# Two banded layers on one core: the second bias added in the first layer's pass, variance work off VectorE, GpSimd's chain in pieces, an order for each layer

## The chip, the cores and the metric

The kernel runs on one core of a Trainium2 chip. The metric is device time in microseconds, the median of several executions. All data is float32.

## The reference

Two layers with the same structure and weights of their own follow each other. Each normalises its input by groups of two channels over the whole 512 x 512 picture, runs a gated banded product over it, and adds the result to its input.

```python
def _ref(x, ...):                     # x: (1, 512, 512, 64)
    xn = _ln(x, norm_scale, norm_bias)
    left = (xn @ Wl + bl) * mask * sigmoid(xn @ Wlg + blg)      # 64 -> 128
    right = (xn @ Wr + br) * mask * sigmoid(xn @ Wrg + brg)
    out_gate = sigmoid(xn @ Wog + bog)
    out = _banded_ingoing(left, right, 4)     # out[i, j] = sum over |d| <= 4 of left[i+d, i] * right[i+d, j]
    out = _ln(out, out_norm_scale, out_norm_bias) * out_gate
    return out @ Wo + bo                                        # 128 -> 64

x = x + _ref(_gn(x), layer 0's weights)   # _gn: mean and variance of each pair of channels
x = x + _ref(_gn(x), layer 1's weights)
```

## The kernel before

First comes a pass over x for the group statistics (`input_stats`), during which the weights of both layers are prepared (`solve_layer`). Then `layer` runs twice, from x to mid_x and from mid_x to out, with `mid_stats` between them, which turns sums gathered on TensorE during the first layer (`sums`) into the second layer's group statistics.

The picture is cut into 9 blocks of 64 rows that overlap by the band, and each block into 2 chunks of columns, so 18 chunks. A chunk has 16 steps, and each step takes one unit of 64 rows x 8 columns in each half of the picture (128 partitions, tile z). A layer has 288 steps of projections, and 288 of outputs, which lag 30 steps behind (`LAG`).

What a unit passes through: it is loaded (`load`), scaled by ga and moved by gb (`affine`, GpSimd), its mean and variance are taken (`inner_stats`, VectorE), it is centred and rescaled (`inner_norm`, GpSimd), transposed on TensorE (`transposed`), evacuated to zT by ScalarE (`kept`), and projected twice (`right`, TensorE; `right_gate`, a sigmoid on ScalarE; `right_end`, a product on VectorE into RO). When a chunk's RO is filled, `mix` multiplies it with the band matrices A on TensorE, in 16 pieces per chunk, and each piece is copied back to RO by one ScalarE and one VectorE copy. Then come the statistics of the outputs (`out_stats`, VectorE), their normalisation (`norm`, eight ScalarE activations of 128x128 per step), the turn to channels on partitions (`turned`, TensorE), the product with the gate (`gates`, `gated`, `times_gate`), the last product with Wo (`end`), and the sum with the residual row XR (`ended`, VectorE). Before that sum, GpSimd has added the layer's bias to XR (`biased`).

Every fourth step `solve` turns the variances gathered since into reciprocal roots: VectorE prepares the variances in tile var, with four small instructions, and makes a first guess in rs by integer arithmetic (`rsqrt`'s first instruction, called the seed here); GpSimd then refines it in ten small instructions, and two more give each output's scale and shift.

All engines keep program order (`InOrder`): each engine executes its instructions in the order in which the loop in `layer` issues them. The loop issues a step's parts in one fixed order, the same for both layers. Two tables spread the uneven work over 16 steps: `count` says how many units GpSimd scales and moves in each step, and `step` gives the band products, two, one or none to a step:

```python
step = [t0 + n for n, k in enumerate((2, 1, 2, 2, 1, 2, 1, 2, 2, 1)) for _ in range(k)]
count = [1, 1, 2, 1, 2, 1, 1, 2, 1, 1, 1, 0, 1, 1, 0, 0]
```

[...] In both layers a pool of two double banks (`two_banks`) serves the projections and the transposes; single banks (`one_bank`) serve the gates, the turn, the last product and the bands: three of them in the first layer, where one more bank gathers the sums, and four in the second. DMAs of the loop are issued from SyncE.

Of the kernel before, what the change touches and what calls it, by code (L numbers as in the profile page):

```python
# [30 lines left out]
LN_EPS = 1e-6  # L31

# [47 lines left out]
def tile_two_banded_layers(  # L80
# [35 lines left out]
    nc.vector.memset(all_ones, 1.0)  # L116
    ones_row = const.tile([1, P], F32, name="ones_row")
# [16 lines left out]
    def rsqrt(o: bass.AP, v: bass.AP, vec=nc.vector, e=nc.vector):  # L134


        p, n = v.shape
        t, u = (
            sm.tile([P, 3 * NB], F32, tag=f"rsqrt{i}", name="rsqrt", bufs=1)[:p, :n]
            for i in range(2)  # L140
        )
        vec.tensor_scalar(
            o.bitcast(I32), v.bitcast(I32), -0.5, float(0x5F3759DF), ALU.mult, ALU.add
        )
        e.tensor_tensor(t, o, o, ALU.mult)
        e.tensor_tensor(t, t, v, ALU.mult)
        e.tensor_scalar(u, t, -10.0 / 3.0, None, ALU.add)
        e.tensor_tensor(t, t, u, ALU.mult)
        e.tensor_scalar(t, t, 5.0, None, ALU.add)
        e.tensor_tensor(o, o, t, ALU.mult)  # L150
        e.tensor_tensor(t, o, o, ALU.mult)
        e.tensor_tensor(t, t, v, ALU.mult)
        e.tensor_scalar(t, t, -27.0 / 1024.0, 0.5625, ALU.mult, ALU.add)
        e.tensor_tensor(o, o, t, ALU.mult)


    PARTS = (
        ("right", 2 * H), ("left", 2 * H), ("gate", H), ("Wo", D), ("ob", 1), ("add", 2 * D),
# [60 lines left out]
    def solve_layer(i: int, f: dict, r: dict, tmp, half: bass.AP):  # L219
# [36 lines left out]
        add = r["add"].rearrange("p (t c) -> p t c", c=D)  # L256
        nc.vector.tensor_copy(add[:, 0, :], pb[:, :D])
# [15 lines left out]
        nc.vector.tensor_tensor(r["m2"], r["m"], r["m"], ALU.mult)  # L273

# [7 lines left out]
    def shifted(i: int, r: dict, tmp):  # L282
        add = r["add"].rearrange("p (t c) -> p t c", c=D)
        if i == 0:

            bias = tmp.tile([P, G], F32, name="bias")
            nc.vector.tensor_reduce(
                bias, add[:, 0, :].rearrange("p (g t) -> p g t", t=2), AX.X, ALU.add
            )
            nc.vector.scalar_tensor_tensor(bias, bias, 0.5, total, ALU.mult, ALU.add)  # L290
            spread(shift, bias)
        op = ALU.add if i else ALU.subtract
        nc.vector.tensor_tensor(add[:, 0, :], add[:, 0, :], shift, op)
        nc.vector.tensor_copy(add[:, 1, :], add[:, 0, :])


# [6 lines left out]
    shift = const.tile([P, D], F32, name="shift")  # L303
# [4 lines left out]
    def group_affine(mean: bass.AP, var: bass.AP, pool):  # L308

        ve = pool.tile([P, D], F32, name="g_ve")  # L310
        nc.vector.tensor_scalar(ve, var, GN_EPS, None, ALU.add)
        rsqrt(ga, ve)
        nc.vector.scalar_tensor_tensor(gb, mean, -1.0, ga, ALU.mult, ALU.mult)
# [113 lines left out]
    def affine(u: Unit, engine):  # L427

        engine.tensor_tensor(u.z, u.z, mid(ga, JU), ALU.mult)
        engine.tensor_tensor(u.z, u.z, mid(gb, JU), ALU.add)  # L430
# [5 lines left out]
    def inner_norm(u: Unit):  # L436
        z = u.z.rearrange("p (k t) c -> p k t c", t=2)
        m = u.mean.unsqueeze(3).broadcast_to([P, JU // 2, 2, D])
        en.gpsimd.tensor_tensor(z, z, m, ALU.subtract)
        en.gpsimd.tensor_tensor(u.z, u.z, last(u.rs, D), ALU.mult)  # L440
# [126 lines left out]
    def mix(c: int, A: bass.AP, h0: int) -> list:  # L567
# [6 lines left out]
        ph = [one_bank().rearrange("i (h t j) -> i h t j", h=q, t=2) for s in range(2)]  # L574
# [23 lines left out]
    def solve(w: dict, ins: list, outs: list, sti, sto):  # L598
# [3 lines left out]
        r = sm.tile([P, 3 * NB], F32, tag="rs", name="rs", bufs=3)[:, : ni + no]  # L602
        if ni:
            en.vector.tensor_scalar(
                v[:, :ni].rearrange("p (k t) -> p k t", t=2), sti[:, : ni // 2, 2::3],
                1.0 / D, LN_EPS, ALU.mult, ALU.add,
            )
            for n, u in enumerate(ins):
                u.rs = r[:, n * JU : (n + 1) * JU]
        if no:  # L610
# [3 lines left out]
            en.vector.scalar_tensor_tensor(  # L614
                vo.rearrange("p (k t) -> p k t", t=2), sto[:, :, 2::3], 1.0 / H,
                w["m2"][:, js].rearrange("p (k t) -> p k t", t=2), ALU.mult, ALU.mult,
            )
            en.vector.tensor_scalar(vo, vo, LN_EPS, None, ALU.add)
            nm = sm.tile([P, NB], F32, tag="nm", name="nm")[:, :no]
            en.vector.tensor_scalar(  # L620
                nm.rearrange("p (k t) -> p k t", t=2), sto[:, :, 1::3], -1.0, None, ALU.mult
            )
        rsqrt(r, v, en.vector, en.gpsimd)
        if no:
            ro = r[:, ni:]
            en.gpsimd.tensor_tensor(ro, ro, w["m"][:, js], ALU.mult)
            en.gpsimd.tensor_tensor(nm, nm, ro, ALU.mult)
            for n, o in enumerate(outs):
                o.rs, o.nm = ro[:, n * JU : (n + 1) * JU], nm[:, n * JU : (n + 1) * JU]

    def norm(o: Out, lo: int, hi: int):
        if lo == 0:
            o.on = onp.tile([P, JU, H], F32, tag="on", name="on")
        for j in range(lo, hi):
            en.scalar.activation(
                o.on[:, j, :].rearrange("p (h t) -> p h t", t=2), RO[:, :, o.c + j, :],
                AF.Identity, bias=o.nm[:, j : j + 1], scale=o.rs[:, j : j + 1],
            )
# [59 lines left out]
    def biased(o: Out, w: dict, stats: bool):  # L698
        n = S + o.blk.m
        f = o.xr[:n, :, 1 : 1 + 2 * D]  # L700
        add = fewer if stats and o.blk.m < S - WIN else w["add"]
        en.gpsimd.tensor_tensor(f, f, mid(add[:n], JU // 2), ALU.add)

    def end(o: Out, w: dict):
        m = o.blk.m
# [33 lines left out]
    def layer(src: bass.AP, dst: bass.AP, w: dict, stats: bool, then=None):  # L739
# [59 lines left out]
        A, sti, sto, then_affine = {}, {}, None, []  # L799
        for t in range(min(loads), last_t + 3):  # L800
# [21 lines left out]

            mixing, mixed = mixes.get(t, []), []
# [10 lines left out]

# [3 lines left out]
            for v in looking[0:3]:  # L838
                out_stats(*v)
            for u in inputs(t + 2):  # L840
                inner_norm(u)
            if t in units:
                right(units[t], 0, w)
            if t in units:
                right_gate(units[t], 0)
            if t in outs:
                gates(outs[t], w)
            if t in units:
                right(units[t], JQ, w)
            for u in affines.pop(t, []):  # L850
                affine(u, en.vector if u.at < NU + 4 else en.gpsimd)
            if t % 4 == 0 and t > NU:
                then_affine = affines.pop(t + 1, [])
            for v in looking[3:5]:
                out_stats(*v)
            for v in looking[5:]:
                out_stats(*v)
            for v in todo:
                inner_stats(*v)
            if t % 4 == 0:  # L860
                st, us = sti.pop((t + 4) // 4, (None, []))
                so, os = sto or (None, [])
                sto = None
                if us or os:
                    solve(w, us, os, st, so)
            if t in outs:
                gated(outs[t])
            if t in units:
                right_end(units[t], 0)
            if t in outs:  # L870
                biased(outs[t], w, stats)
            if t in outs:
                turned(outs[t], w)
            if t in units:
                right_gate(units[t], JQ)
            for u in inputs(t + 1):
                transposed(u)
            if t in outs:
                times_gate(outs[t], w)
            for u in then_affine:  # L880
                affine(u, en.gpsimd)
            then_affine = []
            if t - 1 in outs:
                end(outs[t - 1], w)
            if t in units:
                right_end(units[t], JQ)
            if len(mixing) > 0:
                c, h0 = mixing[0]
                mixed.append(mix(c, A[c, h0 // HA], h0))
            if t + 1 in outs:  # L890
                norm(outs[t + 1], 0, 4)
            for u in inputs(t + 1):
                kept(u)
            if stats and t - 2 in outs:
                sums(outs[t - 2], t - 2 == first_t, t - 2 == last_t)
            if len(mixing) > 0:
                en.scalar.copy(*mixed[0][0])
            if t - 1 in outs:
                ended(dst, outs[t - 1])
            if t + 1 in outs:  # L900
                norm(outs[t + 1], 4, 8)
            if len(mixing) > 1:
                c, h0 = mixing[1]
                mixed.append(mix(c, A[c, h0 // HA], h0))
            if len(mixing) > 0:
                en.vector.tensor_copy(*mixed[0][1])
            if len(mixing) > 1:
                en.scalar.copy(*mixed[1][0])
            if len(mixing) > 1:
# [137 lines left out]
```

## Time and profile before

| | |
|---|---|
| time, median of 3 runs | 4812.61 us (4811.29 to 4815.13) |
| the profiled execution | 4808.51 us, span 4806.5 us |
| busy: PE, weight loads, DVE, ACT, POOL | 3796.6, 3293.0, 3929.9, 3708.4, 3817.1 us |
| mean granted TensorE clock | 0.948 |
| DMA | 983.63 MB, mean 205 GB/s |
| layer 1's outputs, steady part | about 700 to 2300 us |
| layer 2's outputs, steady part | about 2900 to 4500 us |

PE is TensorE's matmul, DVE VectorE, ACT ScalarE, POOL GpSimd, SP SyncE. The program records every instruction through a helper, so all stand on one line (L373) and are told apart by the tiles they write and read: "z<-z,ga" is the scaling of a unit, "z<-z,gb" the moving, "z<-z,sti" the centring, "z<-z,rs" the rescaling, "XR<-XR,pack" (or "fewer") the bias, "var", "rs" and "rsqrt" the solve, "on<-RO" the output normalisation. "A <- B" in the list of waits means that A stood idle until B was done. Busy times and durations are of one profiled execution.

### The profile page before, as it was taken

The numbers are of one execution on the slowest core, as the hardware profiler recorded it, in microseconds if no ns is written. First come the engines' busy times: TensorE is split into PE (matmuls) and PEld (weight loads), VectorE is DVE, ScalarE is ACT, GpSimd is POOL, SyncE is SP. The second block draws the span as 40 slices with busy tenths as digits, with TensorE's granted clock in tenths as the row PEclk, the third lists the DMA queues.
The fourth block names the chain that finished last, engine by engine and source line by source line (L and its number), as shares of the span: only waits on it lengthen the run. The fifth ranks groups of instructions, "written<-read, shape, count | busy, mean of one in ns | idle before, by whom it ended". The sixth has DMA issues, their size and how long they took to land. (4 is left out here: it accounts for less than half of the span.)

```text
span 4806.5 us, 193543 instructions
## 1 busy us (share of the span) xinstructions
PE 3796.6 (79%) x76306; PEld 3293.0 (69%) x76306; DVE 3929.9 (82%) x9635; ACT 3708.4 (77%) x8732; POOL 3817.1 (79%) x4739
## 2 busy tenths in 40 slices
PE   1025799989999999999985478888888888888888
PEld 0024688878888887888854467777777777777775
DVE  6954788888888888888867478888888888888887
ACT  0013689888888898989883268888888888888899
POOL 0035999999999999999734589999999999999964
PEclk9997999999999999999997689999999999999999
DMA  7859677777777777777763967777777777777876
GB/s 299 336 178 108 172 212 213 215 210 215 211 209 210 211 214 212 214 212 215 199 170 100 105 168 212 216 214 209 217 213 215 213 213 218 210 216 211 222 200 179
DMA packets 1437651, 983.63 MB, mean 205 GB/s; under 512 B 167202, under 2 KB 1284424, under 8 KB 1432392
## 3 DMA queue, kind: packets, MB, share of 16 engines
q1 hardware_dynamic: 1432064, 969.75, 73.6%
q8 instruction: 604, 9.90, 0.9%
q14 instruction: 303, 2.48, 0.2%
q10 hardware_dynamic: 4680, 1.50, 0.1%
HBM read 658.42 MB, written 312.46 MB: 202 GB/s over the span
## 5 line engine op out<-in xcount | busy, mean ns | idle before, releaser
L373 ACT ACTIVATE on<-RO,nm,rs 128x128 f32<-128x128 f32 x4608 | 1927.7, 496 | 15.3 <-PE bank L373 9.9
L373 PEld LDWEIGHTS banks<-pack,zT 64*128 64x128 f32 x18576 | 1251.3, 195 | 549.5 <-ACT zT L373 288.9
L373 PE MATMUL banks<-pack,zT 64*128 64x128 f32 x18576 | 1365.6, 289 | 272.8 <-ACT zT L373 222.6
L373 DVE TENSOR_TENSOR RO<-banks,sg 128x512 f32<-128x512 f32 (+1 forms) x1188 | 795.3, 673 | 228.3 <-POOL sg L373 116.2
L373 DVE SCALAR_TENSOR_TENSOR ZH<-bank,pack,gate 128x448 f32<-128x448 f32 (+1 forms) x1152 | 741.6, 685 | 173.3 <-PE bank L373 97.3
L373 ACT ACTIVATE sg<-banks 128x512 f32<-128x512 f32 (+1 forms) x1188 | 698.0, 589 | 188.6 <-PE banks L373 188.2
L373 DVE BATCH_NORM_STATS2 sto<-RO 128x6 f32<-128x256 f32 x2304 | 800.8, 411 | 3.7
L373 POOL TENSOR_TENSOR z<-z,gb 128x512 f32<-128x512 f32 x536 | 684.8, 1278 | 42.0
L373 PE MATMUL bank<-RO,A 64*64 64x128 f32 x18432 | 706.0, 292 | 3.9 <-ACT RO L373 2.4
L373 PE MATMUL bank<-pack,ZH 128*64 128x64 f32 x18432 | 694.6, 231 | 5.0 <-ACT gate L373 4.1
L373 POOL TENSOR_TENSOR z<-z,ga 128x512 f32<-128x512 f32 x536 | 685.6, 1279 | 3.2 <-DMA z<-mid_x 1.9
L373 POOL TENSOR_TENSOR z<-z,rs 128x512 f32<-128x512 f32 x586 | 619.3, 1057 | 46.0
L373 DVE COPY RO<-bank 128x512 f32<-128x512 f32 x576 | 398.4, 692 | 310.6 <-PE bank L373 307.3
L373 PEld LDWEIGHTS bank<-pack,ZH 128*64 128x64 f32 x18432 | 612.6, 143 | 47.3 <-ACT gate L373 8.5
L373 POOL TENSOR_TENSOR z<-z,sti 128x512 f32<-128x512 f32 x586 | 627.9, 1072 | 0.0
L373 PEld LDWEIGHTS bank<-RO,A 64*64 64x64 f32 x18432 | 582.0, 142 | 43.0 <-ACT RO L373 4.1
L373 ACT ACTIVATE gate<-bank 128x448 f32<-128x448 f32 (+1 forms) x1152 | 565.8, 545 | 34.5 <-PE bank L373 32.0
L373 ACT ACTIVATE zT<-banks 128x512 f32<-128x512 f32 (+1 forms) x1084 | 463.5, 481 | 139.6 <-PE banks L373 128.9
L373 PE MATMUL bank<-zg,pack 64*128 64x448 f32 (+1 forms) x2304 | 564.3, 556 | 4.6 <-DMA zg<-later 4.6
L373 ACT COPY RO<-bank 128x512 f32<-128x512 f32 x576 | 333.2, 579 | 282.3 <-PE bank L373 282.1
L373 PE MATMUL banks<-ident,z 64*128 64x64 f32 x4336 | 254.1, 233 | 359.2 <-DVE RO L373 336.9
L373 DVE BATCH_NORM_STATS2 sti<-z 128x6 f32<-128x128 f32 x2344 | 500.5, 280 | 15.2 <-POOL z L373 14.2
(144 smaller groups left out, 3908.6 us busy)
## 6 DMA issues: line engine op xcount, KB each, us to landing
later<-zT SPq DMA_DIRECT2D x576, 256.0 KB
A<-left_of SPq DMA_DIRECT2D x1152, 128.0 KB
zg<-later SPq DMA_DIRECT2D x576, 256.0 KB
z<-in_x_dram SPq DMA_DIRECT2D x576, 128.0 KB
z<-mid_x SPq DMA_DIRECT2D x576, 128.0 KB
gn_x<-in_x_dram SPq DMA_DIRECT2D x16, 4096.0 KB
XR<-in_x_dram SPq DMA_DIRECT2D x448, 112.0 KB
mid_x<-XR SPq DMA_DIRECT2D x448, 112.0 KB
```

The costliest lines, as they stand in the source:

```text
L373: return lambda *a, **k: tc.keep_in_program_order(f(*a, **k))
```

## The change

Four things are changed.

1. Layer 1's pass adds both layers' output biases to the residual (`both` in place of the layer's own), so that mid_x holds the second bias already and layer 2 has no `biased` step. `mid_stats` takes the second bias out of the gathered sums again. Layer 1 no longer subtracts a common shift from mid_x.
2. In `solve`, the units' variances go to ScalarE (an activation with scale and bias), the outputs' variances to GpSimd (two instructions; the factor 1/128 is put into m2 beforehand), and the negated means to ScalarE. On VectorE the seed alone is left.
3. GpSimd's scale and move, its centring and rescaling, and the root's steps are issued as separate parts, which can stand apart in the order.
4. The order of a step's parts is a list, one for each layer. In layer 1 a band piece takes one double bank in place of two single ones (`APART`).

```diff
+APART = (False, True)
+NV = (0, 0)
+FIRST = [
+    "inner stats", "gates", "scale", ("project", 0), ("out stats", 2), "gated",
+    ("out stats", 3), ("project", 4), "turn", "centre", ("sigmoid", 0), "move",
+    "scale next", ("out stats", 99), "solve", "bias", ("solve on", "p"), ("right", 0),
+    "last product", "rescale", ("solve on", "a"), ("sigmoid", 4), ("norm", (0, 4)),
+    ("solve on", "d"), "transpose", ("roots", 2), ("right", 4), ("band", 0), "keep",
+    ("copy a", 0), ("band", 1), ("roots", 2), "sums", ("copy a", 1), ("roots", 2),
+    "norm columns", ("roots", 2), ("roots", 99), "times gate", "move next", ("copy b", 0),
+    ("copy b", 1), ("norm", (4, 8)), "end",
+]
+SECOND = [
+    ("out stats", 2), "gates", "centre", ("out stats", 3), ("project", 0), ("project", 4),
+    ("sigmoid", 0), "scale", "rescale", "gated", ("out stats", 99), "inner stats",
+    ("right", 0), "solve", "turn", "scale next", "last product", ("solve on", "p"),
+    ("solve on", "a"), ("solve on", "d"), "transpose", ("sigmoid", 4), "move", ("roots", 2),
+    "times gate", "end", ("roots", 2), ("band", 0), ("norm", (0, 4)), "norm columns",
+    ("roots", 2), ("roots", 2), "keep", ("right", 4), ("copy a", 0), ("band", 1),
+    ("roots", 99), ("norm", (4, 8)), ("copy b", 0), "move next", ("copy a", 1),
+    ("copy b", 1),
+]
+ORDERS = (FIRST, SECOND)
...
-    def affine(u: Unit, engine):
-
+    def scaled(u: Unit, engine):
         engine.tensor_tensor(u.z, u.z, mid(ga, JU), ALU.mult)
+
+    def moved(u: Unit, engine):
         engine.tensor_tensor(u.z, u.z, mid(gb, JU), ALU.add)
...
+        if APART[0 if stats else 1]:
+            pb = [one_bank() for s in range(2)]
+        else:
+            two = two_banks()
+            pb = [two[:, s * 512 : (s + 1) * 512] for s in range(2)]
...
-            en.vector.tensor_scalar(
-                v[:, :ni].rearrange("p (k t) -> p k t", t=2), sti[:, : ni // 2, 2::3],
-                1.0 / D, LN_EPS, ALU.mult, ALU.add,
+            of = sti[:, : ni // 2, 2::3]
+            act.append(
+                lambda: en.scalar.activation(
+                    pairs(v[:, :ni]), of, AF.Identity, bias=ln_eps, scale=1.0 / D
+                )
             )
...
-            en.vector.scalar_tensor_tensor(
-                vo.rearrange("p (k t) -> p k t", t=2), sto[:, :, 2::3], 1.0 / H,
-                w["m2"][:, js].rearrange("p (k t) -> p k t", t=2), ALU.mult, ALU.mult,
-            )
-            en.vector.tensor_scalar(vo, vo, LN_EPS, None, ALU.add)
             nm = sm.tile([P, NB], F32, tag="nm", name="nm")[:, :no]
-            en.vector.tensor_scalar(
-                nm.rearrange("p (k t) -> p k t", t=2), sto[:, :, 1::3], -1.0, None, ALU.mult
-            )
-        rsqrt(r, v, en.vector, en.gpsimd)
+            act.append(lambda: en.scalar.mul(pairs(nm), sto[:, :, 1::3], -1.0))
+            pool += [
+                lambda: en.gpsimd.tensor_tensor(
+                    pairs(vo), sto[:, :, 2::3], pairs(w["m2"][:, js]), ALU.mult
+                ),
+                lambda: en.gpsimd.tensor_scalar(vo, vo, LN_EPS, None, ALU.add),
+            ]
+        seed, *todo = rsqrt(r, v, en.vector, en.gpsimd)
...
+        return {"a": act, "p": pool, "d": [seed], "roots": todo}
...
-    def biased(o: Out, w: dict, stats: bool):
+    def biased(o: Out, w: dict):
         n = S + o.blk.m
         f = o.xr[:n, :, 1 : 1 + 2 * D]
-        add = fewer if stats and o.blk.m < S - WIN else w["add"]
+        add = fewer if o.blk.m < S - WIN else both
         en.gpsimd.tensor_tensor(f, f, mid(add[:n], JU // 2), ALU.add)
```

The loop over a step's parts in `layer` is replaced by one over the list; each name stands for the part of the same kind before ("band" is `mix`, "copy a" and "copy b" its ScalarE and VectorE copies, "last product" is `end`, "end" is `ended`, "turn" is `turned`, "solve on" issues the variance work of ScalarE ("a"), GpSimd ("p") and the seed ("d"), "roots" so many of GpSimd's refining instructions). "scale next" and "move next" treat, in every fourth step, the units of the step after, as before. `NV` is zero in both layers, so "norm columns" issues nothing.

## The prediction

> **What bounds the kernel now.** I read the busy times by stretch first, then the groups of instructions with shapes apart and the list of waits, each for the same two stretches of 1000 us in mid-layer (1000 to 2000 us, layer 1; 3200 to 4200 us, layer 2), and the timeline last. Columns of the stretches: start, end and length, then for PE, PEld, DVE, ACT and POOL busy time and instructions, the granted clock, the DMA share and GB/s.
>
> ```profile
> 1000.00:2000.00 1000.00, 915.40 (x19402) 808.53 (x19400) 853.16 (x2101) 890.67 (x2073) 917.87 (x1103) 0.98 0.76 211
> 3200.00:4200.00 1000.00, 841.95 (x17340) 739.23 (x17340) 888.88 (x2133) 875.49 (x2094) 927.56 (x1119) 0.96 0.77 213
> ```
>
> Every engine is busy 84 to 93%, so shares decide nothing; the waits do. Waits of layer 2 (who, for whom, us in total, times, longest), and of POOL in layer 1 last:
>
> ```profile
> PE banks L373 <- DVE RO L373: 112.1, 92, 3.9
> ACT RO L373 <- PE bank L373: 80.1, 61, 2.9
> DVE RO L373 <- PE bank L373: 57.0, 132, 1.2
> ACT zT L373 <- PE banks L373: 42.3, 18, 2.8
> PE banks L373 <- ACT zT L373: 36.7, 47, 1.3
> POOL rsqrt L373 <- DVE rs L373: 18.5, 24, 1.7
> ...
> POOL rsqrt L373 <- DVE rs L373: 29.3, 34, 1.9
> ```
>
> PE, ACT and DVE wait for each other; POOL waits for one thing only, VectorE's first step of the root, 18.5 and 29.3 us of 1000. Its other idle time is the pause behind an instruction that needs the one before. POOL sets the pace of both layers.
>
> A step does two gate activations: 276 of them in the first stretch make 138 steps of 7.25 us, 279 in the second 7.17 us. Taking each engine's own waits off in layer 2 leaves its own work per step: POOL 7.17 - 18.5/139.5 = 7.03 us; DVE (waits 105.5) 6.41; ACT (waits 123.3) 6.28; PE (waits 156.8) 6.04. Layer 1: POOL 7.25 - 0.21 = 7.03. The groups that the change touches, layer 2 (busy us, mean ns | idle before):
>
> ```profile
> L373 POOL TENSOR_TENSOR z<-z,gb 128x512 f32<-128x512 f32 x142 | 181.5, 1278 | 11.1
> L373 POOL TENSOR_TENSOR XR<-XR,pack 120x512 f32<-120x512 f32 x139 | 165.4, 1190 | 0.2
> L373 POOL TENSOR_TENSOR z<-z,rs 128x512 f32<-128x512 f32 x138 | 143.9, 1043 | 10.8
> L373 DVE TENSOR_SCALAR var<-var 128x32 f32<-128x32 f32 x35 | 24.6, 702 | 1.2
> L373 DVE TENSOR_SCALAR var<-sti 128x32 f32<-128x32 f32 x35 | 24.1, 687 | 0.0
> L373 DVE TENSOR_SCALAR rs<-var 128x64 int32<-128x64 int32 x35 | 16.1, 461 | 0.0
> ```
>
> **Layer 2, the bias.** One XR add per step goes: 165.4/139 = 1.19 us. With it gone, mid_x already holds the second bias, and the sum that closes a step waits for the loaded row alone.
>
> **The variance work, both layers.** A solve comes every four steps. VectorE loses four small instructions: var<-sti 24.1, var<-var 24.6, var<-sto 6.5, nm 6.0 us, 61.2/35 = 1.75 us per solve, 0.44 per step. ScalarE gains two of 128x32. The trace has none of that size on ACT: its 128x128 norm takes 0.50 us, VectorE's nm of 128x32 0.17; I take 0.3 each (0.15 per step, bounds 0.09 to 0.25), queued between the first sigmoid and the second. POOL gains a product and an addition of 128x32: nearest are its nm (0.25) and a 128x64 scalar step (0.33), with pauses of 0.08, so 0.65 per solve, 0.16 per step.
>
> **The chain in pieces.** z is now scaled, another unit centred, then z moved: an instruction no longer follows the one it needs. The pauses before gb and rs go, (11.1 + 10.8)/139.5 = 0.16 per step. If independent neighbours do not close up as the groups with 0.0 idle do, this is 0. The small root steps stay back to back, so their pauses stay.
>
> POOL's own work: layer 1 7.03 + 0.16 - 0.16 = 7.03, unchanged; layer 2 7.03 - 1.19 + 0.16 - 0.16 = 5.84. So in layer 2 the late one is next ACT, 6.28 + 0.15 = 6.43, before PE 6.04 and DVE 6.41 - 0.44 = 5.97.
>
> **The seed's new wait.** Now VectorE's first root step (rs<-var) must wait for POOL's two new instructions. In layer 1 these stand behind scale, centre, move, scale next and bias of the same step: with one unit 1.28 + 1.06 + 1.28 + 1.28 + 1.19 = 6.1 us into POOL's step, and VectorE reaches the seed after about 3 us (statistics 1.40 + 0.87, one product 0.69). Behind the seed on VectorE are the second right product, the gate product, the band copies and the closing sum; PE's band, which now takes the double bank that the second right product frees, waits for these, and ACT's band copy for PE. This costs nothing as long as POOL is the late one anyway, and POOL itself waits only from its second instruction to the seed, behind one rescale of 1.04 us. On the other side, POOL must now wait in each solve for VectorE's statistics, before the chain, where formerly it could run on. I take 0.2 per step in all for layer 1, as much as now (0.21), bounds 0.05 to 0.5.
>
> How long the seed takes is seen in the timeline:
>
> ```profile
> 1507.27 1.27 POOL L373 TENSOR_TENSOR z<-z,ga 128x512 f32<-128x512 f32 x1
> 1507.62 0.97 DVE L373 TENSOR_SCALAR var<-sti 128x32 f32<-128x32 f32 x1
> 1508.62 1.26 POOL L373 TENSOR_TENSOR z<-z,gb 128x512 f32<-128x512 f32 x1
> 1508.72 1.20 DVE L373 TENSOR_SCALAR var<-var 128x32 f32<-128x32 f32 x1
> ```
>
> Two 32-column steps that take 0.16 us elsewhere ended as POOL's did. The seed is of this kind and now starts behind a POOL instruction of 1.04 (layer 1) or 1.28 us (layer 2): up to 1.1 us in place of 0.2 to 0.46, per solve at most 0.2 us per step, inside the bounds above.
>
> [...]
>
> **The orders.** Layer 2's keeps ACT's sequence as it is and VectorE's but for the closing sum ahead of the second product; PE takes the last product ahead of the transposes. In the light steps (no band) of the present order ACT already runs without a gap, gate to gate 3522.41 - 3516.74 = 5.67 us, with POOL out of the way. So the order permits ACT's pace. With bands PE, ACT and DVE each need about 6.8 us in a two-band step, and some waiting stays. Of ACT's 0.88 us of waits per step I keep a third, 0.27: 6.43 + 0.27 = 6.70 us. Bounds: 6.45 (no waits) and 7.05 (most stay: the heaviest four steps hold 6 of 16 affine units, so POOL there needs 6 x 2.56 + 4 x 2.1 + 4.5 + 0.65 = 28.9 us, where 4.5 is the root's chain in the timeline, against ACT's 4 x 5.67 + 6 x 0.58 + 0.6 = 26.8). SyncE is near too: 10 DMA issues per step (2 each of z, XR, stores and A, one of later and zg in the list of issues) of about 0.6 us each in the timeline, and the DMA share 0.77 rises to 0.82. In layer 1 bands move from the single banks to the double ones: PE's 915.4 us over 138 steps is 6.63 us, below POOL, so that is covered; were it not, PE would be next with 6.6 plus waits.
>
> The setup loses the per-layer shift and mid_stats gains six small VectorE steps between the layers, some 2 us each way: 0. The filling and draining (0 to 700, 2300 to 2900, from 4500) keep their pace.
>
> **Sum.** Steady layer 1 is 700 to 2300 us, 1600/7.25 = 221 steps; steady layer 2 is 2900 to 4500, 223 steps. Layer 2: 223 x (7.17 - 6.70) = -105 us. Layer 1: 7.03 + 0.20 = 7.23 against 7.25, -0.02 x 221 = -4 us. The profiled execution took 4808.5 us (span 4806.5), so 4699.5; it lies 4.1 us under the median of 4812.6, so I state 4704.
>
> **Rivals.**
> B, the gain is small: in layer 2 seed and POOL are locked to each other at every solve, the heavy steps stay with POOL and SyncE, and steps stop at 7.0. 223 x 0.17 = 38 us less, layer 1 unchanged: 4775. For it: the 28.9 against 26.8. Against: POOL's sum over 16 steps falls well below ACT's.
> C, slower: in layer 1 VectorE's stand at the seed is not covered. If PE and ACT, idle meanwhile, need longer than POOL's next four steps to make up, every solve adds. With 2.8 us in each of 55 solves, 154 us, against 105 from layer 2: 49 us slower, 4862. It decides from 105/55 = 1.9 us per solve. For it: the stand of 3 us and more, and PE's 6.63. Against: four steps of POOL are 28 us, VectorE's own work 24.
> The bias cannot fail to leave layer 2; that VectorE is freed may bring nothing in either case, since it is bound in neither layer.
>
> **Chances.** Forecast 0.57 (own range 4640 to 4755), B 0.21, C 0.18, a tie 0.04. Faster by over 0.2% (about what a measurement here can tell from no change): 0.57 + 0.21 = 0.78; within 0.2% 0.04; slower 0.18. Low end: 6.45 in layer 2 (-161) and 7.08 in layer 1 (-38) give 4614; both together are rare, so 4635. High end: half of C's stall lies near 4800; with 4825 about 0.16 is left out above.
>
> **What would show it.** No XR add on POOL in layer 2, POOL's busy share there near 85%, ACT's near 93%; steps of 6.7 us by the gate activations. In layer 1 POOL still near 92%, steps 7.2, and the wait "DVE rs <- POOL var" new and long while POOL's own waits stay near 0.2 us per step. Wrong, if layer 1's step is over 7.5, or if in layer 2 POOL still waits least.

## The result: slightly slower, and the profile after

Twenty runs of each kernel: 4830.09 us after the change, 4814.25 us before. The ratio is 1.0035 with a 95% interval of 1.0027 to 1.0043, where 0.977 had been forecast. The medians differ by 15.8 us. The two profiled executions lie further apart, with spans of 4835.9 and 4806.5 us: the one of the changed kernel is 7.6 us over its median, the other 5.7 us under its own. So the table below shows some 13 us more loss than the medians do.

Where these 29.4 us lie is read from the starts of the gate activations, the first and the last of each layer (us):

| | to the first gate of layer 1 | layer 1, first to last gate | between the layers | layer 2, first to last gate |
|---|---|---|---|---|
| before | 539.7 | 2015.3 | 272.9 | 1970.7 |
| after | 522.2 | 2093.8 | 268.6 | 1943.6 |
| difference | -17.5 | +78.5 | -4.3 | -27.1 |

Layer 2 gained a quarter of what was forecast, and layer 1, forecast to stand still, lost nearly three times that gain. The mean step in mid-layer went from 7.15 to 7.07 us in layer 2, and from 7.22 to 7.54 in layer 1. These means hide where the time lies in layer 2. By the place of a step in its chunk (0 to 15, from one step's gate to the next one's, mean of 14 chunks), the two longest steps before, 4 and 8, went from 11.7 and 11.5 us to 6.6 and 8.1; two others grew, step 6 from 6.7 to 10.6 and step 11 from 5.7 to 8.8.

The busy times by stretch, after, in the columns explained in the prediction:

```profile
1000.00:2000.00 1000.00, 913.37 (x18584) 796.45 (x18583) 776.87 (x1886) 864.10 (x2061) 887.39 (x1131) 0.95 0.73 202
3200.00:4200.00 1000.00, 876.26 (x17552) 756.81 (x17550) 841.69 (x2016) 898.30 (x2195) 787.06 (x1060) 0.96 0.79 216
```

In layer 2 POOL (the fifth busy time) went from 927.56 to 787.06: the bias did leave it. In layer 1 it went from 917.87 to 887.39, though POOL has no less to do there: something holds up the engine that set the pace. The waits of layer 2 after, the two that PE and POOL have on transfers and what follows from them on ACT and VectorE:

```profile
POOL z L391 <- DMA z<-mid_x: 134.7, 42, 7.2
DVE RO L391 <- ACT sg L391: 109.3, 53, 6.0
ACT sg L391 <- PE banks L391: 92.2, 69, 5.9
PE bank L391 <- DMA zg<-later: 71.7, 28, 4.6
```

POOL now stands for the load of a unit (z), up to 7.2 us at once, and PE for the gate's input (zg), the first TensorE work of a step. Before, no engine waited for a load in this stretch. The waits of layer 1, where POOL had waited for VectorE's seed alone, now have POOL's two largest as:

```profile
POOL XR L391 <- DMA XR<-in_x_dram: 36.3, 23, 4.2
POOL z L391 <- DMA z<-in_x_dram: 21.4, 14, 2.5
```

These too are loads that come late. The loads of both layers pass through SyncE's one queue, in program order with the stores. SyncE's timeline in a band-heavy step of layer 2, after (start, us, engine, transfer, number of issues):

```profile
3605.05 0.55 SPq L391 DMA_DIRECT2D zg<-later  x1
3605.70 0.82 SPq L391 DMA_DIRECT2D out_dram<-XR  x2
3606.62 0.55 SPq L391 DMA_DIRECT2D later<-zT  x1
3607.27 3.26 SPq L391 DMA_DIRECT2D z<-mid_x  x4
3610.58 1.02 SPq L391 DMA_DIRECT2D XR<-mid_x  x2
3611.72 2.88 SPq L391 DMA_DIRECT2D A<-left_of  x4
3615.01 0.34 SPq L391 DMA_DIRECT2D zg<-later  x1
```

Fourteen issues stand one behind the other from 3605.05 to 3614.60, 9.55 us in a step that should last 6.7; the next zg is issued behind them, and PE waits 3.87 us for it, until 3618.24. What SyncE itself waits for in layer 1, first before, then after:

```profile
SPq L373 <- DVE XR L373: 8.2, 13, 1.4
```

```profile
SPq L391 <- DVE XR L391: 61.7, 33, 3.9
```

"DVE XR" is the sum that closes a step ("end"). FIRST puts it last on VectorE; its store to mid_x is issued from SyncE ahead of the next step's loads, so SyncE stands at the store, and the loads of z, XR and zg stand behind it. The same wait in layer 2, before, then after:

```profile
SPq L373 <- DVE XR L373: 4.5, 6, 1.4
```

```profile
SPq L391 <- DVE XR L391: 52.3, 39, 3.7
```

It grew there too, though SECOND has the sum ahead of the band copies. No run issues layer 2's store later under SECOND, so what this wait costs isn't known; it may follow from the late loads as well as cause them.

The groups that the change added, layer 1 after:

```profile
L391 ACT ACTIVATE var<-sti,ln_eps 128x32 f32<-128x32 f32 x33 | 11.5, 349 | 0.0
L391 POOL TENSOR_SCALAR var<-var 128x32 f32<-128x32 f32 x33 | 9.5, 288 | 2.9
L391 POOL TENSOR_TENSOR var<-sto,pack 128x32 f32<-128x32 f32 x33 | 8.9, 270 | 0.0
L391 DVE TENSOR_SCALAR rs<-var 128x64 int32<-128x64 int32 x33 | 6.4, 195 | 64.6 <-POOL var L391 61.9 <-ACT zT L391 2.5
```

The sizes of the new instructions were met: 0.35 us on ACT where 0.3 was taken (the other one, nm, 0.26), 0.27 + 0.29 and a pause of 0.09 on POOL where 0.65 was taken, and the idle time before gb is 0.0. The last line is the seed: VectorE stands 61.9 us of 1000 ahead of it, for POOL, as foretold.

### The profile page after: what moved, and what is told of

Read it like the earlier page. It is cut to its first block, busy times and chain, and to the rows that moved or that the text cites. A ratio compares the mean times of both kernels' runs of the same rounds, so it can differ in the third digit from the quotient of the medians.

```text
span 4835.9 us, 192971 instructions
## 1 busy us (share of the span) xinstructions
PE 3899.5 (81%) x76306; PEld 3340.4 (69%) x76306; DVE 3737.4 (77%) x9061; ACT 3749.9 (78%) x9022; POOL 3530.7 (73%) x4739
## 3 DMA queue, kind: packets, MB, share of 16 engines
q14 instruction: 299, 2.45, 0.2%
## 4 chain that ended last, share of the span: by engine, by line
PE 35%; ACT 16%; DMA 11%; POOL 11%; issue 9%; DVE 6%; SPq 4%; POOLq 0%; DVEq 0%; ACTq 0%
PE bank L391 17%; PE banks L391 16%; ACT on L391 9%; POOL z L391 7%; SPq L391 4%; DMA zg<-later 3%; DMA XR<-in_x_dram 3%; ACT gate L391 2%; PE acc L391 2%; ACT zT L391 2%; ACT sg L391 2%; DMA z<-mid_x 2%; POOL rsqrt L391 2%; DVE RO L391 1%; DVE sto L391 1%
## 5 line engine op out<-in xcount | busy, mean ns | idle before, releaser
L391 PEld LDWEIGHTS banks<-pack,zT 64*128 64x128 f32 x18576 | 1288.9, 203 | 431.7 <-ACT zT L391 250.6
L391 PE MATMUL banks<-pack,zT 64*128 64x128 f32 x18576 | 1321.8, 291 | 213.7 <-ACT zT L391 175.7
L391 PE MATMUL bank<-zg,pack 64*128 64x448 f32 (+1 forms) x2304 | 684.9, 622 | 194.9 <-DMA zg<-later 123.0
L391 PE MATMUL bank<-pack,ZH 128*64 128x64 f32 x18432 | 665.7, 225 | 13.1 <-ACT gate L391 11.8
L391 PEld LDWEIGHTS bank<-pack,ZH 128*64 128x64 f32 x18432 | 585.9, 138 | 57.3 <-ACT gate L391 22.0
L391 DVE BATCH_NORM_STATS2 sti<-z 128x6 f32<-128x128 f32 x2344 | 501.7, 280 | 11.6 <-POOL z L391 5.9
L391 PE MATMUL bank<-ident,on 64*128 64x64 f32 x9216 | 450.4, 227 | 41.2 <-ACT gate L391 27.2
L391 PEld LDWEIGHTS bank<-ident,on 64*128 64x128 f32 x9216 | 415.4, 141 | 92.4 <-ACT gate L391 37.0
L391 PE MATMUL banks<-RO,A 64*64 64x128 f32 x9216 | 338.0, 289 | 105.9 <-DVE RO L391 99.2
L391 PEld LDWEIGHTS bank<-zg,pack 64*128 64x128 f32 x2304 | 221.6, 193 | 276.5 <-issue 67.3
L391 DVE TENSOR_TENSOR XR<-bank,XR 120x512 f32<-120x512 f32 (+1 forms) x576 | 391.2, 679 | 1.5 <-PE bank L391 0.8
```

What stands on the lines that cost most here:

```text
L391: return lambda *a, **k: tc.keep_in_program_order(f(*a, **k))
```

## The experiments

All start from the changed kernel. A list OLD puts its named parts into the order of the kernel before, and OLD_SECOND is OLD without the bias and the sums, for layer 2. "VectorE variance" means that part 2 of the change is undone (all four preparing instructions back on VectorE). Layer times and mean steps (in mid-layer) are those of each run's profiled execution, as above. The median of the kernel before differs by chip (4814 to 4838), so ratios are to the runs of before on the same chip, and layer times of different chips are compared to some 10 us only.

| run | ratio to before, 95% | layer 1 | layer 2 | step 1 | step 2 |
|---|---|---|---|---|---|
| e1 bias alone | 0.9856 (0.9839 to 0.9873) | 2005.7 | 1931.5 | 7.17 | 7.02 |
| e2 parts 1, 2 | 0.9914 (0.9897 to 0.9931) | 2032.0 | 1936.8 | 7.25 | 7.01 |
| e3 e2 + SECOND | 0.9921 (0.9900 to 0.9943) | 2031.0 | 1944.4 | 7.25 | 7.04 |
| e4 single banks | 1.0269 (1.0254 to 1.0284) | 2211.3 | 1945.5 | 7.96 | 7.07 |
| e5 half rows | 0.9808 (0.9787 to 0.9828) | 2002.1 | 1887.8 | 7.15 | 6.83 |
| e6 zg from ACT | 0.9917 (0.9902 to 0.9932) | 2009.6 | 1955.3 | 7.19 | 7.08 |
| e7 A from POOL | 1.0148 (1.0130 to 1.0166) | 2006.2 | 2039.9 | 7.19 | 7.41 |
| e8 FIRST, VectorE variance | 1.0021 (1.0008 to 1.0034) | 2094.4 | 1926.5 | 7.54 | 7.01 |
| e9 FIRST, store late | 0.9949 (0.9932 to 0.9966) | 2048.9 | 1929.4 | 7.32 | 6.98 |
| e10 FIRST, end early | 0.9955 (0.9936 to 0.9974) | 2053.3 | 1940.6 | 7.40 | 7.03 |
| e11 e1 + zg first | 0.9798 (0.9783 to 0.9812) | 2013.6 | 1893.3 | 7.24 | 6.85 |
| e12 e1 + store late | 0.9990 (0.9979 to 1.0001) | 2030.5 | 1986.1 | 7.25 | 7.11 |
| e13 change + zg first | 1.0133 (1.0117 to 1.0148) | 2112.4 | 1963.6 | 7.64 | 7.15 |
| e14 e13 + end early | 1.0054 (1.0039 to 1.0069) | 2077.6 | 1961.7 | 7.53 | 7.14 |
| e15 OLD, SECOND, zg first | 0.9941 (0.9926 to 0.9956) | 2020.0 | 1965.3 | 7.26 | 7.16 |
| e16 e11 + earlier loads | 0.9953 (0.9936 to 0.9969) | 2051.5 | 1902.7 | 7.39 | 6.89 |
| e17 change + earlier loads | 1.0050 (1.0031 to 1.0068) | 2088.6 | 1941.5 | 7.51 | 7.04 |
| e18 e17 + zg first | 1.0021 (1.0006 to 1.0036) | 2120.7 | 1888.9 | 7.69 | 6.82 |

### e1 to e4: the change taken apart

```diff
 e1, VectorE variance and
+APART = (True, True)
+ORDERS = (OLD, OLD_SECOND)
 e2, the change's variance work and
+APART = (True, True)
+ORDERS = (OLD, OLD_SECOND)
 e3, the change's variance work and
+APART = (True, True)
+ORDERS = (OLD, SECOND)
 e4, all of the change but
+APART = (True, True)
```

> Part 1 alone: the second bias added in layer 1's pass; variance work on VectorE and the order of the kernel before in both layers. If SyncE's queue is what holds layer 2 (loads of z and zg land late once GpSimd has room), layer 2's steps stay at 7.0 to 7.1 us and the time is about 4785. If it is the new order of layer 2 that wastes the room, the steps here come to 6.7 to 6.8 and the time to about 4710. Layer 1 is as before in either case (7.2 us a step).

> Parts 1 and 2: the bias and the variance work moved, with the order of the kernel before in both layers and the bands in single banks. If FIRST's order is the cause of layer 1's loss, layer 1's steps are 7.2 to 7.3 us here; if the two instructions that GpSimd gains are, 7.4 or more. Layer 2 within 0.1 us of the bias alone if SyncE holds it.

> As the changed kernel, but layer 1 in the order of the kernel before, with bands in single banks. If FIRST costs layer 1 its 78 us, the time is about 4770; if the loss comes with the moved variance work, it stays over 4810.

> The changed kernel, but layer 1's bands in single banks as before. If the bands' double banks tie PE to VectorE, layer 1's steps fall from 7.5 to about 7.2 us and the time to about 4770; if the cause is the seed's place behind GpSimd's two instructions, or late loads, both stay within 0.1 us and 15 us of the changed kernel.

The bias alone gains 1.44%, the variance work on top costs 0.58%, SECOND's order changes nothing that its interval can tell, and FIRST's costs the rest: 1.0035 - 0.9914 = 1.2% (1.1% against e3). By layers: the variance work adds 26 us in layer 1 (2005.7 to 2032.0) and 5 in layer 2, and FIRST adds 62 in layer 1 (2032.0 to 2093.8). The double banks for the bands are not to blame for that: with single ones FIRST takes 2211, so they save 117 us under this order. The shares of 26 and 62 us hold for this order of taking the change apart. In the other order, from e1 to e8 (below), FIRST costs 89 us, and the variance work nothing on top of it (2094.4 and 2093.8).

In layer 2 every order of these runs ends at 1930 to 1945 us. The limit is common to them, and it isn't POOL, busy 779 us of 1000 in e1. Waits of e1 in layer 2:

```profile
PE bank L401 <- DMA zg<-later: 46.0, 30, 3.2
...
POOL z L401 <- DMA z<-mid_x: 44.5, 18, 5.0
```

ACT, the busiest engine, is at 897 us of 1000, and the same two loads are late. POOL's longest wait in e1 is another one, for VectorE's seed:

```profile
POOL rsqrt L401 <- DVE rs L401: 117.5, 35, 7.3
```

POOL has run ahead of VectorE there; in e11, which is faster, this wait is 56.1 us.

### e5, e6, e7, e11, e12, e16: what makes the loads late in layer 2

```diff
 e5, on e1
-    en.sync.dma_start(o.xr[rows, :, 1 : 1 + 2 * D], rows_of(src, o, e))
+    k = JU // 2 if src is x else JU // 4
+    en.sync.dma_start(o.xr[rows, :k, 1 : 1 + 2 * D], rows_of(src, o, e)[:, :k])
...
 e6, on e1: layer 2's zg is issued from ScalarE's queue, behind "gated"
-    en.sync.dma_start(o.t, later[o.at])
+    q.dma_start(o.t, later[o.at])
 e7, on e1: the transfers of A
-    en.sync.dma_start(A[...], ...)
+    (en.sync if stats else en.gpsimd).dma_start(A[...], ...)
 e11, on e1
+    if t + 2 in outs:
+        recall(outs[t + 2])          # the load of zg
     for u in loads.get(t, []):       # the loads of z
         load(src, u)
-    if t + 2 in outs:
-        recall(outs[t + 2])
 e12, on e1: a step's stores of mid_x or out are issued in the next step, behind its loads
 e16, on e11
-    loads.setdefault(ahead[t] - 2, []).append(u)
+    loads.setdefault(ahead[t] - 3, []).append(u)
```

> The bias alone, and in layer 2 the residual rows XR are loaded and the outputs stored for half of their columns only (the other half of the output is left out): as many DMA issues as before, some 15% fewer bytes per step. If the DMA engines' bandwidth holds layer 2 (share 0.8 to 0.9 in its heavy steps), steps fall from 7.02 to 6.8 us or less; if it is the rate at which SyncE issues (10 issues of 0.6 us per step), they stay within 0.06 us.

> The bias alone, and in layer 2 the load of zg is issued by ScalarE's queue behind the gate activations, in place of SyncE's: 9 issues per step on SyncE for 10, 0.5 us more on ScalarE. If SyncE's queue holds layer 2, PE's wait for zg goes and the steps fall to 6.8 to 6.9 us (about 35 us less in all); if not, ScalarE's 0.5 us shows and the steps stay at 7.0 or grow.

> The bias alone, and in layer 2 the loads of the band matrices A (2 issues per step on average, 4 to a step in the heavy ones) are issued by GpSimd in place of SyncE. If SyncE's queue holds layer 2 and an issue costs GpSimd under 0.5 us, the steps fall to 6.7 to 6.8 us; if an issue costs GpSimd 1 us or more, GpSimd is back at 7.0 or beyond and the time grows.

> The bias alone, with the load of zg as the first issue of a step on SyncE, ahead of z, XR and the band matrices, in both layers. If layer 2's remaining loss is only zg's place in the queue, PE's wait for it goes and steps fall from 7.02 to about 6.9 us (some 30 us less in all); if the queue and the DMA engines are full, the lateness moves on to z or A and the time stays within 10 us.

> The bias alone, with the store of a finished row issued after the next step's loads in both layers. Its order has the closing sum early, so little is gained: within 15 us of the bias alone if SyncE's issue rate and the DMA engines are what is left, 30 us or more below it if the wait at the store still is.

> The bias alone with zg first, and z loaded three steps ahead of its scaling in place of two. If the loads are only late, GpSimd's wait for them goes and layer 2 falls by 15 us or more from 1893; if SyncE and the DMA engines are full in the heavy steps, it stays within 10 us.

e5 has e1's number of transfers with fewer bytes (half of the output stays unwritten), and layer 2 takes 44 us less; e11 has e1's transfers and bytes with zg ahead of z, and takes 38 less. The profiled execution of e5 is 24 us under the median of its four, so 44 is a high figure: by the ratios e5 is 0.5% (23 us) below e1, and e11 0.6% (28 us). Layer 2 of e5, then of e11:

```profile
3200.00:4200.00 1000.00, 862.10 (x18278) 753.19 (x18276) 885.15 (x2242) 921.27 (x2204) 803.56 (x1032) 0.99 0.69 191
```

```profile
3200.00:4200.00 1000.00, 863.49 (x18086) 756.10 (x18080) 889.97 (x2226) 914.00 (x2184) 799.51 (x1023) 0.98 0.81 223
```

The two waits for loads in e11:

```profile
POOL z L401 <- DMA z<-mid_x: 75.2, 24, 7.3
...
PE bank L401 <- DMA zg<-later: 4.1, 5, 1.8
```

The DMA share falls to 0.69 in one and rises to 0.81 in the other, for nearly the same step: bytes count, the place in the queue counts as much, and where zg arrives in time ACT comes up to 92 and 91%. e11 changes nothing but that place, and PE's wait for zg falls from 46.0 to 4.1 us. So the loads did hold layer 2, and ACT, the engine forecast as the next bound, is reached only behind them.

The other three show what a way round SyncE costs. e6 takes zg out of SyncE's queue; both late loads vanish (POOL's wait for z is 3.0 us of 1000, PE's for zg is gone), but PE's wait for ScalarE's zT, which now stands behind the issues, rises from 47.1 us (e1) to 91.1, and the layer takes 24 us more than e1's: the 6.8 to 6.9 expected per step was missed, 7.08. e7 gives POOL two more instructions per step, 268 issues of 0.62 us in the 1000; its busy time goes from 779 to 901, it waits for nothing but the seed (50.3 us), and it is the bound again at 7.41 us. e12 was expected to change little and lost 1.3% against e1: the late store holds its XR tile longer, and SyncE waits 75.1 us (layer 1) and 77.7 us (layer 2) of 1000 for the stores to land. e16 issues the loads of z three steps ahead in place of two. It takes POOL's wait for z away (2.9 us) and gains nothing for it: layer 2 is 1902.7 against 1893.3, and layer 1 and the start lose 38 and 26. So under this order the late z stood in POOL's slack, and zg was what counted.

### e8, e9, e10: FIRST in layer 1

```diff
 e8, VectorE variance and
+ORDERS = (FIRST, OLD_SECOND)
 e9, the change's variance work, ORDERS = (FIRST, OLD_SECOND), and in layer 1
-    for e in range(2):
-        en.sync.dma_start(rows_of(dst, o, e), ...)
+    def store(): ...                 # called in the next step, behind its loads
 e10, the change's variance work and
+FIRST_E = [x for x in FIRST if x != "end"]
+FIRST_E.insert(FIRST_E.index("times gate") + 1, "end")
+ORDERS = (FIRST_E, OLD_SECOND)
```

> Layer 1 in the order FIRST with the variance work back on VectorE, layer 2 as in the bias alone. If the seed's stand behind GpSimd's two instructions is what makes FIRST slow, layer 1 comes back from 2094 to about 2030 us between its first and last gate; if it is the late loads and the rest of the order, it stays over 2070.

> The changed kernel with layer 2 in the order of the kernel before, and in layer 1 the store of a finished row issued only after the next step's loads, so that SyncE no longer waits for VectorE's closing sum ahead of them; no engine's own order is changed. If FIRST is slow because that wait holds up the loads of z and XR behind it, layer 1 falls from 2094 us (first to last gate) to about 2040, and GpSimd's waits for these loads go. If not, it stays over 2080.

> FIRST with the closing sum moved on VectorE from the last place to behind the gate product, ahead of the band copies; layer 2 in the order of the kernel before. If the late store holds up SyncE's loads, layer 1 falls to about 2040 us as with the later store; if PE's wait for the band copies is the larger part (these now come later still), it stays over 2080.

e8 asks whether it is the seed, whose stand is gone with the variances back on VectorE. Layer 1 takes 2094.4 us, the changed kernel's 2093.8. That doesn't make the stand of 61.9 us of 1000 free, for in its place VectorE executes the four preparing instructions again, 72.1 us in e8:

```profile
L401 DVE TENSOR_SCALAR var<-var 128x32 f32<-128x32 f32 x33 | 25.6, 775 | 1.1
L401 DVE TENSOR_TENSOR var<-sto,pack 128x32 f32<-128x32 f32 x33 | 23.6, 716 | 1.1
L401 DVE TENSOR_SCALAR var<-sti 128x32 f32<-128x32 f32 x33 | 13.7, 415 | 0.0
L401 DVE TENSOR_SCALAR nm<-sto 128x32 f32<-128x32 f32 x33 | 9.2, 280 | 0.0
```

The first two take 437 and 439 ns in e1; in e8 some end with the GpSimd instruction beside them, as in the prediction's four rows (var<-sti at 1358.67 takes 0.97 us, to within 0.03 us of the end of GpSimd's scaling). The steps show the exchange: against the changed kernel, e8 is 1.7 us shorter at step 12, and at the other three solves, steps 0, 4 and 8, 1.4 us longer in all. So e8 shows that the variance work under FIRST costs the same on either side; what the stand costs by itself stays open. SyncE's wait in e8, layer 1, is what stayed:

```profile
SPq L401 <- DVE XR L401: 59.1, 38, 4.1
```

e9 and e10 take this wait away in two ways, by issuing the loads ahead of the store, and by taking the closing sum from the last place. SyncE's waits in layer 1 of e9:

```profile
SPq L401 <- DMA mid_x<-XR: 65.9, 72, 3.5
```

The wait for the sum is practically gone there (0.6 us) and another one has come, for earlier stores to land before their tile is loaded anew; in e10 the wait for the sum is halved (30.3). Layer 1 falls by 45 and 41 us, to 2048.9 and 2053.3. So some two thirds of FIRST's 62 us come from the closing sum's place ahead of the loads. e14 against e13 (below) agrees: with the sum moved forward SyncE's wait for it falls from 86.2 to 29.6 us, and layer 1 by 35. The rest, 17 and 21 us, wasn't settled. In e9 it stands in steps 11 to 13, which together take 4.5 us longer than in e2, partly made up in the other steps. In the changed kernel steps 12 and 13 together take 15.8 us, where e2 has 11.6 and e8 14.1; at the solve of step 12 POOL waits about 1.5 us for z, and the seed 2.6 us for POOL.

### e13 to e15, e17, e18: the repairs put together

```diff
 e13: the change and e11's edit
 e14: e13 with FIRST_E in place of FIRST
 e15: ORDERS = (OLD, SECOND), APART = (True, True), VectorE variance, e11's edit
 e17: the change and
-    loads.setdefault(ahead[t] - 2, []).append(u)
+    loads.setdefault(ahead[t] - (2 if stats else 3), []).append(u)
 e18: e17 and e11's edit
```

> The changed kernel with zg loaded as the first issue of each step on SyncE, nothing else. If the place in SyncE's queue is what holds layer 2 under SECOND, its steps fall from 7.07 to 6.9 us (some 35 us less in layer 2); layer 1, whose loss is the store's wait ahead of z and XR, gains under 15 us.

> As e13, and in layer 1 the closing sum ahead of the band copies. If both places in SyncE's queue explain the orders' loss, layer 1 is at 2040 to 2055 us and layer 2 as in e13, the time near 4765; if the orders cost by themselves, it stays over 4790.

> The bias moved, variance work on VectorE, layer 1 in the order of the kernel before, layer 2 in SECOND, zg first in the queue. If SECOND costs nothing by itself, layer 2 is within 15 us of the 1893 us that the order of before gave with zg first; if its order ties ACT and PE closer, 30 us or more above.

> The changed kernel, with z loaded three steps ahead of its scaling in place of two in layer 2 only. If late loads of z hold layer 2 under SECOND, GpSimd's wait for them goes and layer 2 falls from 1944 to 1900 us or less; if the queue and the DMA engines are simply full, or the order itself is the limit, the wait turns up elsewhere and layer 2 stays over 1930.

> As e17, with zg as the first issue of each step. If lateness of z and zg together is the limit, layer 2 falls to 1890 us or less, the figure of the order of before with zg first; if the order itself is the limit it stays over 1930.

The gains that e13, e14 and e15 looked for didn't come: under SECOND, zg first makes layer 2 slower (1962 to 1965). e13 gained in neither layer; e14 and e15 came out as their expectations have it for an order that costs by itself, which e18 then answers for layer 2. The waits of e13 in layer 2:

```profile
POOL z L391 <- DMA z<-mid_x: 147.8, 43, 7.5
DVE rs L391 <- POOL var L391: 96.9, 26, 8.8
```

z, now one place further back, is late for POOL (147.8 us, 134.7 after the change), and VectorE's stand at the seed, behind POOL, grows from 13.4 to 96.9 us, which undoes what PE gains on zg (71.7 to 2.2). e15 has no such stand and is as slow, so the stand isn't the only way in which POOL's lateness is passed on. e17 is the counterpart. Its waits in layer 2:

```profile
POOL var L391 <- DVE sto L391: 122.0, 27, 6.4
...
PE bank L391 <- DMA zg<-later: 71.4, 32, 4.3
```

The wait for z is down to 4.8 us, as intended, but the time is the same (1941.5): PE's wait for zg is what it was, and POOL now stands for VectorE's statistics instead. Only with both repairs, in e18, does the layer move. Its waits for the two loads:

```profile
POOL z L391 <- DMA z<-mid_x: 80.9, 29, 6.4
...
PE bank L391 <- DMA zg<-later: 37.0, 22, 4.2
```

After the change they were 134.7 and 71.7; SyncE's wait for the closing sum fell with them, from 52.3 to 7.7. Layer 2 takes 1888.9 us, 55 less than after the change, 6.82 per step. So under SECOND the two late loads hold the layer together, and taking away either one leaves the other. The whole kernel is still no faster than before (1.0021), since zg first lengthens layer 1 under FIRST to 2120.7, where SyncE's wait for the closing sum grows to 81.3 us of 1000.

The best of all runs is e11, the bias alone with zg first: 4730.17 us, 0.9798 (0.9783 to 0.9812), faster than both kernels.

## Why the prediction was wrong

**Layer 2, what the bias brings.** Right in its mechanism: POOL was the bound, one add of 1.19 us per step left it, and it gained slack. Wrong in what is late next, and this is the first failed step. The sum named ACT by comparing the engines' own work, and took SyncE as "near too" without a price, though it had counted 10 issues of about 0.6 us and a DMA share going from 0.77 to 0.82. It should have been a row of that comparison: 10 x 0.6 = 6.0 us on average, which alone would still stand below ACT's 6.43, and 9.55 us in the step shown above, which stands far over it. The heaviest steps were reckoned for POOL (28.9 us in four), and not for SyncE. Once POOL ran ahead, the loads came late. Step 6.70 forecast, 7.07 measured: 223 x 0.37 = 83 us. What the loads' lateness is worth is shown by e11 under the old order (6.85) and by e18 under the new one (6.82); the other 0.12 to 0.15 us above the forecast lie in what was left for waits: ACT is busy 6.34 us of e18's 6.80 in the stretch, so it idles 0.46 where 0.27 had been left. (A third of 0.88, as the prediction says, would have been 0.29.)

**Layer 1, the orders.** This is the second failed step, and the one behind layer 1's loss; by these sizes the change would have come out faster with either step right. The prediction followed PE's banks and the seed through FIRST, but not SyncE's queue behind the moved closing sum: "end" moved on VectorE from ahead of the band copies to the last place, and what it issues, the store, stands ahead of the next loads. The place of the sum was looked at for layer 2, whose order has it earlier, and not for layer 1. The loss under FIRST is 62 us from e2, some two thirds of it from this; what makes up the rest stays open.

**The variance work.** The sizes were right and the net was off, in a term that the sum put at nothing. POOL's added 0.16 per step was to be paid for by 0.16 from the pieces; with the pieces together (e2) it costs 0.08 per step and 26 us in layer 1, half of the 0.16 x 288 = 46 us that it would be if nothing hid it. The pause before gb did vanish with the pieces, but under FIRST POOL is no longer what sets the pace, so that gain can't be seen. That VectorE is relieved of 0.44 us per step brings nothing in either layer, as said.

**The seed.** The new wait was foretold, and it is there. Rival C priced it at 2.8 us a solve. e8 takes the stand away, but puts VectorE's own work of about the same length in its place, so it neither shows that price nor rules it out. C was right on the sign and on the layer; the store's place, which explains most of the loss, isn't in it. For the instruction itself the prediction allowed up to 1.1 us in its new place, an estimate from two other VectorE steps that ended as POOL's did. The seed took 195 ns on average in layer 1, where 196 ns had been measured before, and 475 ns in layer 2, where it had been 461 ns. So in its new place it was not longer in layer 1, and 14 ns longer in layer 2.

**Rival B** had the size for layer 2 (7.0 per step, against 7.07), and one of its two reasons, SyncE; its other one, POOL held in the heavy steps by its own work, is refuted: the two steps that POOL held before fell from 11.7 and 11.5 us to 6.6 and 8.1, and e18 gives POOL the same work and takes 6.82 a step.

**The start** had been put at 0 and gave 17.5 us less to the first gate, and 8 to 17 less in all the runs but e16, against the one trace of the kernel before; why was not tried. "Between the layers" was right at 0 to within 5 us.

**The marks** that would show it wrong did: layer 1's step over 7.5 (7.54). POOL's share in layer 2 was to be near 85% and fell to 79, ACT's near 93 and stopped at 90.

## What to carry to other kernels

Treat a queue that issues transfers in program order as one more engine (here SyncE's, with 14 issues in 9.55 us of a heavy step): give it a row in the comparison of own work, in the heavy steps too, before naming the next bound. When an order moves a step, look up what that step issues into such a queue and what stands behind it; here a store that waited for a sum at the end of a step delayed the next step's loads, and cost 41 to 45 us. An experiment that takes a wait away and puts work of the same length in its place doesn't price the wait. And where two late loads hold a stage together, removing one may show nothing or even a loss (layer 2 took 1941.5 and 1963.6 us with one repair, 1888.9 with both, 1943.6 without): try both before dropping the theory.

## What the runs showed of the hardware

The granted TensorE clock fell to 0.50 after idle times of PE of 2.34 us in the changed kernel and 1.73 us in the kernel before. The timeline of the changed kernel in layer 1 (start, us, engine, operation; in brackets the idle time before and its releaser):

```profile
1358.65 0.20 DVE L391 TENSOR_SCALAR rs<-var 128x64 int32<-128x64 int32 x1 [2.28 <-POOL var L391]
...
1360.09 2.45 PE L391 MATMUL bank<-zg,pack 64*128 64x448 f32 x4 [2.34 <-DVE ZH L391]
...
1361.75 3.78 PE L391 MATMUL banks<-pack,zT 64*128 64x128 f32 x30
```

The granted clock there, by stretch:

```profile
1358.00:1362.00 4.00, 1.91 (x6) 1.55 (x8) 3.35 (x10) 2.36 (x7) 3.41 (x10) 0.71 0.87 232
1362.00:1366.00 4.00, 4.00 (x42) 4.00 (x41) 1.68 (x5) 1.68 (x3) 3.52 (x9) 0.50 0.66 181
```

PE idles 2.34 us, then four gate products take 2.45 us where most groups of four between 1000 and 2000 us take 1.02 to 1.16, and the clock is at 0.50 for the 4 us after, before it rises again (0.95 over the 6 us from 1366). So this stop cost more than its own length. The fall doesn't always come at once: after the stop of 3.87 us in layer 2 (until 3618.24) the four gate products took 1.02 us, and the clock was 0.67 over the 4 us from 3618. The kernel before has such falls too: behind a stop of 1.73 us, until 1310.28, its clock was 0.50 from 1310.95 to 1314.36. The mean clock of the stretch from 1000 to 2000 us is 0.95 here, 0.98 before and 0.99 in e1. An estimate from these means: 0.03 of 1000 us is 30 us of full clock, so over layer 1's 2094 us at most some 60 us, if nothing hid it. In the rows above the stop follows on the seed's wait of 2.28 us. What decides when the clock falls was not shown by these runs. How much of layer 1's loss is due to the clock was not tried by itself; the mean clock of a whole execution doesn't order the times (the changed kernel's executions at 0.918 took 4815.0, 4819.9 and 4830.0 us, those at 0.943 from 4831.6 to 4840.9).
